# The same transformer kernel, with each engine's instructions ordered by another model of durations

## The chip, the cores and the metric

The program runs on one core of a Trainium2 chip. The metric is device time in microseconds. A core has separate instruction streams that run side by side and meet at semaphores: TensorE (PE, with its weight loads shown as PEld), VectorE (DVE), ScalarE (ACT), GpSimd (POOL) and SyncE (SP). SP here does nothing but issue DMA transfers; POOL issues some too. Within one stream the instructions run in the order in which they stand in the program.

## The reference

Input x has 4 sequences of 512 tokens with 128 channels. Four layers follow, each an attention part and a feed-forward part, with the layer norm behind each sum:

```python
for attn, ffn in layers:            # 4 layers
    x = layernorm(x + attn(x))
    x = layernorm(x + ffn(x))
```

- Layer 0: causal attention, 16 heads of 8 (`softmax(q k^T / sqrt(8) + causal) v`, then a projection); the feed-forward part is itself two small layers of local attention (8 heads of 64, window 64, normalised and rotated q and k) with a gated GELU network each.
- Layer 1: attention with relative positions (16 heads of 8; scores `(q k^T + q r^T + u k^T + v r^T)/sqrt(8)` with the terms in r shifted by row); feed-forward by 8 experts of which 2 are chosen per token.
- Layer 2: attention with a bias that falls linearly with distance (ALiBi), 16 heads of 8; a feed-forward network with ternary weights, 128 to 512 to 512 to 512 to 128.
- Layer 3: attention with 16 heads of 64 and tables of relative keys and values over distances from -16 to 16; feed-forward by 16 experts, 4 of them chosen in groups, and shared ones.

All arrays are float32. The output is x.

## The kernel before, in words

The residual stream x stays on the chip, one tile X per sequence of 128 x 4 x 128. `build` runs eight stages in one program: `Causal` (tiles named a0), `F0`, `Rel` (a1), `F1`, `Alibi` (a2), `F2`, `A3` and `F3`. Each stage is written as Python generators that take turns: `K.step` lets every generator that is open trace one more portion, `K.turn` hands out the PSUM banks for the smaller products, `K.tick` traces the next stage's preparation in the background. So the order in which instructions are traced already interleaves units of work.

That trace order is not yet the program's order. The tile context collects all instructions with their dependencies and then orders each engine's instructions itself. It walks through a modelled machine: at every point, among the instructions of an engine whose inputs the model has ready, it takes the one with the lowest priority number. The number is the place in trace order, which the kernel shifts in places. `K.front(800)`, for instance, puts the value matmuls ahead by 800, and the background has an offset of its own. What "ready" means at each point comes from modelled durations. Buffers of a pool and manual dependencies (`K.waits`, `K.behind`) are edges that any order keeps.

The causal and the ALiBi attention work in 16 units of 4 heads of one sequence:

- `load` (L518, L520): the operand tile Q of 256 KB and four blocks of rows of K of 64 KB each come back from DRAM (`a0iq`, `a0ik`) over SP, into one of `nb = 3` sets of buffers. `prep` had written them there by `spread` (L503) in three parts h, l of the float32 numbers; `ql` (L623) is the lower part. `constant` and `operands` (L479 to L494) fill the constant rows.
- `maxima` (L646 matmul, L648 on DVE): the scores by row, only to take the row maximum.
- `rows_out` (L664): the maxima are transposed, negated into the tile `nm`, and `mrow` (L532) writes them by DMA as one more row of Q, so that the second product of the scores comes out with the maximum subtracted.
- `exp` (L679 matmul into t, L723 exponent on ACT into Pt, L732 causal select on POOL), and the value matmuls (L695 into o), traced with `k.front(800)`. `exp` of a unit is traced only once its `rows_out` has been.

The relative attention `Rel` does the same with maxima at L922 to L927, scores at L996 to L998, the exponent at L999 and L1008, products on POOL at L1014 to L1018 and values at L972. `A3` works on one head of one sequence at a time: operand transfers on SP and POOL (L1235 to L1253; tiles a3Q, a3QT, a3K, a3KT, W), scores at L1285 and L1286, maximum L1290 on DVE, exponent p at L1291 on ACT, transposes by PE (L212 into t), the copy PT at L1304, a write of p to DRAM that is read back by diagonals (L1313 a3dpw, L1317 at), and values at L1334 under `k.front(800)`. `F0` has its projections near L1548 to L1610, scores at L1626, mask and maximum at L1639, exponent at L1641, transposes and copy at L1651, values at L1670, and its gated network at L1702 to L1765. `F1` has its expert outputs at L1952, `F2` its hidden products at L2053, `F3` its hidden part at L2200 to L2211 and its outputs at L2220. Weight tiles are split into an upper and a lower part by `split_w` (load into `wraw`, DVE at L295, POOL at L296), and products of such parts are three matmuls (`mm3`, L302 to L304).

## Time and profile before

| | us |
|---|---|
| median of 3 runs | 2275.97 (2273.09 to 2276.8) |
| profiled execution | 2282.43 |
| its span | 2280.7 |
| PE busy / DVE busy / ACT busy / POOL busy | 2028.8 / 1672.1 / 1333.8 / 589.0 |

The profiled execution is one run with the hardware profiler; its time is 1.7 us more than its span, and 6.5 us (0.28%) above the median. The granted clock of TensorE was 0.954 in it. The span is roughly: start to 55 us, causal attention to 190, F0 to 640, change of stage to 770, relative attention to 1095, F1 to 1255, ALiBi attention to 1455, F2 to 1600, A3 to 2150, F3 to the end. Neighbouring stages overlap at these borders. "Busy" counts the time in which an engine has an instruction in it, a waiting one among pipelined matmuls included; it is not the time at peak.

### The profile page before, as it was taken

What the parts mean: (1) busy time and instruction counts of PE and PEld (TensorE: products, weight loads), DVE (VectorE), ACT (ScalarE), POOL (GpSimd) and SP (SyncE); (2) the same over time, 40 slices, a digit from 0 to 9 for tenths busy, and PEclk for the clock granted to TensorE, in tenths of its full rate; (3) what the DMA queues carried; (4) which work ended last, traced back from release to release, by engine and by line L of the source; (5) the groups of instructions that cost most, each with busy time, mean ns of one, the idle gap of its engine ahead of it and who ended that gap; (6) DMA issues with size and microseconds to landing.
All of it is one profiled execution on the core that took longest, in us unless ns stands there. A gap on an engine that the chain in (4) does not pass through costs nothing.

```text
span 2280.7 us, 42119 instructions
## 1 busy us (share of the span) xinstructions
PE 2028.8 (89%) x13888; PEld 1473.5 (65%) x13888; DVE 1672.1 (73%) x5583; ACT 1333.8 (58%) x2982; POOL 589.0 (26%) x781
## 2 busy tenths in 40 slices
PE   5999787888778899999999999899899999999897
PEld 3666566666555566665788666677566666665676
DVE  4778688688978677874677787452778877778787
ACT  2566786677753456556342566332777776777632
POOL 3222212111222655555200222522111111111221
PEclk9999998899997899988999999999899999999999
DMA  6321311011341543420220330512889978898400
GB/s 183 91 78 34 101 47 47 22 28 30 112 130 54 165 141 116 143 75 23 69 65 9 108 106 30 167 54 57 211 204 217 206 192 184 199 216 197 118 5 15
DMA packets 265507, 242.31 MB, mean 106 GB/s; under 512 B 106368, under 2 KB 190634, under 8 KB 264522
## 3 DMA queue, kind: packets, MB, share of 16 engines
q1 hardware_dynamic: 260058, 222.12, 36.5%
q0 software_dynamic: 5232, 17.50, 3.3%
q8 instruction: 111, 1.82, 0.3%
q14 instruction: 106, 0.87, 0.1%
HBM read 103.03 MB, written 74.32 MB: 78 GB/s over the span
## 4 chain that ended last, share of the span: by engine, by line
PE 50%; DVE 13%; ACT 7%; DMA 5%; POOL 3%; issue 3%; SPq 1%; ACTq 0%; POOLq 0%; DVEq 0%
PE s L2053 4%; PE t L212 4%; PE o L1334 3%; PE o L972 3%; PE o L1952 2%; PE b L302 2%; PE s L302 2%; PE s L646 2%; PE t L679 2%; PE o L695 2%; PE s L303 2%; PE s L304 2%; PE b L303 2%; PE s L1285 2%; PE w L924 2%
## 5 line engine op out<-in xcount | busy, mean ns | idle before, releaser
L927 DVE CUSTOM_DVE_ANT_0 junk<-w,a1mask 128x640 bf16<-128x640 f32 x256 | 203.2, 817 | 67.8 <-PE w L925 66.8
L723 ACT ACTIVATE Pt<-t 128x384 f32<-128x384 f32 (+1 forms) x384 | 179.8, 529 | 74.8 <-PE t L679 62.6
L212 PE MATMUL t<-ident,p 128*128 128x128 f32 x1280 | 202.1, 278 | 21.0 <-ACT p L1291 15.6
L212 PEld LDWEIGHTS t<-ident,p 128*128 128x128 f32 x1280 | 150.8, 141 | 80.6 <-ACT p L1291 37.4
L999 ACT ACTIVATE Pt<-t 128x512 f32<-128x512 f32 x256 | 148.8, 597 | 84.2 <-PE t L998 44.3
L1304 ACT COPY PT<-t 128x512 f32<-128x512 f32 x256 | 149.7, 594 | 76.3 <-PE t L212 72.4
L1291 ACT ACTIVATE p<-s,nb 128x512 f32<-128x512 f32 x256 | 178.0, 700 | 13.0 <-DVE nb L1290 6.9
L1290 DVE TENSOR_REDUCE nb<-s 128x1 f32<-128x512 f32 x256 | 174.5, 685 | 2.5
L648 DVE CUSTOM_DVE_ANT_0 junk<-s,a0mask 128x128 bf16<-128x128 f32 (+3 forms) x256 | 114.0, 485 | 44.0 <-PE s L646 43.2
L1309 DVE CUSTOM_DVE_ANT_0 jk<-p,a3right 128x496 bf16<-128x496 f32 (+3 forms) x256 | 124.2, 485 | 26.9 <-ACT p L1291 16.0
L648 DVE CUSTOM_DVE_ANT_0 junk<-s,a2mask 128x128 bf16<-128x128 f32 (+3 forms) x256 | 114.9, 484 | 29.7 <-PE s L646 29.4
L732 POOL TENSOR_SCALAR_AFFINE_SELECT Pt<-Pt 128x512 f32<-128x512 f32 x112 | 70.9, 645 | 233.5 <-ACT Pt L723 233.4
L1288 DVE TENSOR_TENSOR s<-s,W 128x160 f32<-128x160 f32 (+1 forms) x256 | 80.9, 318 | 65.2 <-PE s L1286 64.3
L1285 PE MATMUL s<-a3KT,a3QT 128*128 128x512 f32 x256 | 118.5, 465 | 9.0 <-DMA a3K<-L 4.3
L1641 ACT ACTIVATE p<-sm,nb 128x128 f32<-128x128 f32 x256 | 100.7, 396 | 30.7 <-DVE nb L1639 30.0
L1334 PE MATMUL o<-PT,V 128*64 128x512 f32 x512 | 116.9, 598 | 0.5 <-ACT PT L1304 0.5
L996 PE MATMUL t<-a1Q,a1K 128*128 128x512 f32 (+3 forms) x256 | 96.5, 385 | 7.9 <-ACT Pt L999 5.3
L1286 PE MATMUL s<-a3K,a3Q 128*128 128x512 f32 x256 | 102.3, 400 | 0.0
L924 PE MATMUL w<-a1K,a1Q 128*128 128x256 f32 (+2 forms) x192 | 85.7, 447 | 14.1 <-DVE mx L927 13.1
L646 PE MATMUL s<-a0K,a0Q 128*128 128x256 f32 (+2 forms) x256 | 82.9, 380 | 16.6 <-DVE mx L648 8.0
L1639 DVE CUSTOM_DVE_ANT_0 sm<-s,band,rn 128x128 f32<-128x128 f32 x256 | 78.2, 343 | 24.1 <-PE s L1626 16.2
L1327 POOL CAST a<-at 128x256 fp32r<-128x256 f32 x32 | 12.9, 402 | 313.0 <-DMA at<-a3dpw 200.6
(494 smaller groups left out, 5927.3 us busy)
## 6 DMA issues: line engine op xcount, KB each, us to landing
W<-a3dsk SPq DMA_DIRECT2D x32, 640.0 KB
a1Q<-a1iq SPq DMA_DIRECT2D x32, 512.0 KB
a3dpw<-p SPq DMA_DIRECT2D x64, 160.0 KB
a3dpw<-p SPq DMA_DIRECT2D x64, 144.0 KB
a1K<-a1ik SPq DMA_DIRECT2D x64, 128.0 KB
a3Q<-a3dim SPq DMA_DIRECT2D x32, 256.0 KB
a3QT<-H SPq DMA_DIRECT2D x64, 128.0 KB
a3QT<-L SPq DMA_DIRECT2D x64, 128.0 KB
```

The lines of the kernel that those rows point to most:

```text
L212: self.nc.tensor.matmul(out.bitcast(x.dtype), x, i[:n, :n], is_transpose=True, start=start, stop=stop)
L646: self.scored = nc.tensor.matmul(s[:, :nm], self.qof(0, t, i)[:, qc * P:(qc + 1) * P], Ks[:, i, :nm], start=True, stop=True).ins
L648: nc.vector.tensor_tensor_reduce(junk[:, :n], s[:, :n], k.mask[:, 512 - n:512], 1.0, NEG, ALU.add, ALU.max, mx[:, qc, i:i + 1])
L723: ready = nc.scalar.activation(Pt[:, i, z:], s[:, z:], AF.Exp, scale=sc).ins
L924: nc.tensor.matmul(s[:, 0, T - n:], self.qof(0, t, i)[:, qs], Ks[:, i, 0:n], start=True, stop=True)
L927: nc.vector.tensor_tensor_reduce(junk, s.rearrange("p a n -> p (a n)")[:, T - n:T + m], k.mask[:, T - n:T + m], 1.0, NEG, ALU.add, ALU.max ...
L999: nc.scalar.activation(Pt[:, i, :T], s, AF.Exp, scale=sc)
L1285: nc.tensor.matmul(s, QT[:, e, qs], KT[:, e, :], start=True, stop=False)
L1290: nc.vector.tensor_reduce(nb, s, AX.X, ALU.min)
L1291: nc.scalar.activation(p[:, e, :], s, AF.Exp, bias=nb, scale=-1.0, accum_out=den[:, qc, 2 * un + e:2 * un + e + 1])
L1304: self.copied[t] = nc.scalar.copy(PT[e][:, :, qc * P:qc * P + P], tb.rearrange("p (c n) -> p c n", n=P)).ins
L1334: m = nc.tensor.matmul(o[64 * e:64 * e + 64, :], V[:, kc, h * 64:h * 64 + 64], PT[e][:, kc, :], start=(kc == 0), stop=False)
```

## The change

One argument is given to the tile context. The context then walks through its modelled machine with its other model of durations (a timeline simulation) when it orders the instructions of each engine. Trace order, priorities, dependencies, tiles and arithmetic stay as they were; which instruction counts as ready at which point, and so the order on each engine and the semaphore waits that go with it, can come out otherwise.

```diff
-    with tile.TileContext(nc) as tc:
+    with tile.TileContext(nc, schedule_with_timeline_sim=True) as tc:
         build(tc, aps, range(8))
```

## The prediction

> **What bounds the kernel now.** I read the page's busy shares first, then the chain that ended last, the waits of PE and last the start of the timeline; the windows by stage gave the sizes.
>
> ```profile
> PE 2028.8 (89%) x13888; PEld 1473.5 (65%) x13888; DVE 1672.1 (73%) x5583; ACT 1333.8 (58%) x2982; POOL 589.0 (26%) x781
> ...
> PE 50%; DVE 13%; ACT 7%; DMA 5%; POOL 3%; issue 3%; SPq 1%; ACTq 0%; POOLq 0%; DVEq 0%
> ```
>
> PE is busy 89% of the span, yet only 50% of the chain is matmul time. The other half is a softmax step on DVE or ACT, a transfer, or the moment before a matmul that nothing explains. So the order in which PE meets results of other engines is worth time, though no engine's work changes.
>
> ```profile
> 1600.00:2150.00 550.00, 514.89 (x2879) 342.60 (x2879) 427.19 (x1247) 409.54 (x962) 71.60 (x127) 0.99 0.84 199
> 190.00:640.00 450.00, 369.82 (x3624) 280.64 (x3623) 362.34 (x1292) 323.39 (x890) 88.67 (x108) 0.93 0.21 54
> ```
>
> Two of the windows (length; PE, PEld, DVE, ACT, POOL busy; clock; DMA share; GB/s): the relative-key attention (A3) leaves PE idle 35 us, the local attention (F0) 80 us of 252 in all. DVE and PE are equally loaded in F0, so an order that is better for PE can be worse for DVE there.
>
> ```profile
> PE t L212 <- ACT p L1291: 15.6, 24, 1.6
> PE s L646 <- DVE mx L648: 14.1, 26, 2.5
> ...
> PE s L646 <- DMA a0K<-a0ik: 7.9, 1, 7.9
> PE b L302 <- DVE ql L623: 7.8, 1, 7.8
> ...
> PE t L679 <- DMA a0Q<-nm: 4.6, 3, 2.6
> ```
>
> PE's waits (us, times, longest): no matmul waits for an operand load of the causal attention (a0Q, a0K) after the first one, and only 3 of 16 units wait for the row of maxima (nm). Those loads are in time now; I watch whether they stay so.
>
> ```profile
> 15.60 0.75 DVE L623 SCALAR_TENSOR_TENSOR ql<-b,a0bqk,qh 128x512 fp32r<-128x512 f32 x1 [8.68 <-DMA a0ik<-a0c]
> 23.81 7.67 SPq L520 DMA_DIRECT2D a0K<-a0ik  x12
> 29.63 2.35 PE L646 MATMUL s<-a0K,a0Q 128*128 128x256 f32 x6 [7.88 <-DMA a0K<-a0ik]
> ```
>
> The start is one dependent run: fills on SP, ql, loads, first maxima at 29.6 us.
>
> **The change, part by part.** It removes and adds no matmul, activation of data or transfer; it permutes each engine's list. Beside that, ACT loads its activation table once more (41 times for 40; such a load takes 1.28 us at L316, and I count it as hidden, ACT being idle 42% of the time; 1.3 if it is not), and the instructions that only wait go from 801 to 690 on PE and from 662 to 695 on SP, which I cost at nothing but their place. I compared the two orders: the matmuls fall into 7799 runs of equal instructions before and 7727 after, the mean matmul moves by 2.3 us of PE work, score matmuls (L646, L924, L1626) come earlier by 3 to 4 us, value matmuls (L972, L1334, L1952, L2220) later by 2 to 4. To price this I give every instruction the mean duration that its group has in the trace and measure **room**: the PE work between the matmul that feeds another engine (or the place where a transfer can be issued) and the matmul that uses the result. Room below the steps in between is **shortfall**, a wait. One late result delays all behind it, so sums of shortfalls overstate; what part I take is judgement.
>
> *Start.* POOL now has two a0K memsets (1.77 us each, from 5.30 for three) ahead of the identity's select (which stood at 1.64), and further memsets ahead of a0wqkl. SP has table and weight loads of F0 ahead of the fills and spreads that ql and the first load wait for. Followed by hand with the rows' durations, ql moves from 15.6 to about 21, the first maxima from 29.6 to about 35. Nothing hides this, PE has no other work. +6 (0 if the transfers overlap, to 10).
>
> *Causal attention.* Maxima run earlier, so each Q load of 256 KB (L518) is needed sooner after its buffer comes free. Room from issue to first use: 3.5 to 9.8 before, median 6.4; after, unit by unit from the fourth, 6.7, 7.3, 5.8, 7.5, 3.9, 1.8, 2.0, 2.5, 2.0, 0.7, 1.1, 0.3, 0.8. The nearest row for such a load is "a3K<-in_c_step_dram POOLq DMA_DIRECT2D x2, 256.0 KB, 5.2", so the shortfalls are 1.3+3.4+3.2+2.7+3.2+4.5+4.1+4.9+4.4 = 32, less about 2 that exist now: 30. PE still has values and exponent matmuls of older units there; I take two thirds, 20. The nm row (L532) needs some 2.1 from issue: the chain shows 2.68, 2.50 and 1.77 for a2Q<-nm. Its room falls from a median of 2.9 to 1.2: 16 x 0.9 = 14, of which 4.6 is paid now; most falls into the same delays, 3 more. +23 (8 if other matmuls cover, 40 if not).
>
> The Trainium skill, "DMA: Bandwidth & Descriptors", section "Anatomy of one DMA — SWDGE (gpsimd) path", fits a transfer as 2.0 us plus its bytes over 436e3. By it the 256 KB load would be an estimated 2.6 us, the shortfalls 10 instead of 32 and this term about +8; the 5.2 us row disagrees, and the row decides. The rule is also one against the change: 2 us that do not shrink are more than the 1.2 of room left to nm.
>
> *Alibi attention.* Q loads keep their room (15.7, now 17). nm's median room falls from 3.3 to 1.6, below 2.1 in about 11 units by 0.6: +7 (0 to 12).
>
> *A3.* Value matmuls stand further behind their last PT copy (room 1.0, now 2.0; the copy is 0.59), transposes behind the exponent 4.0 instead of 3.8. Shortfalls as PE sees them go from 90 to 54 us, as DVE sees them from 125 to 73. But PE's recorded waits for the exponent are only 15.6, and the chain in this stage is 5.9% a3dpw<-p, 5.1% a3Q<-H and 3.2% L1253: loads that a better order of matmuls does not shorten. Their median room grows (a3KT 4.8 to 8.0, a3K 5.5 to 7.9), its lowest tenth shrinks (3.1 to 1.8, 3.6 to 2.8), because SP interleaves loads with writes of p. Of the 36 saved I take a little over half: -20 (-45, with part of DVE's 52, to +5).
>
> *F0.* Transposes after the exponent get 4.4 instead of 2.9; PE's shortfalls fall from 139 to 86, DVE's rise from 173 to 192. The 53 on PE is nearly given back where DVE, as loaded as PE, is the one that waits: -5 (-35 to +20).
>
> *The rest.* Rel: value room 2.9 to 4.0, PE's shortfalls 105 to 116: -3 (-12 to 8). F1's clean alternation of 12 hidden and 8 out matmuls is broken up, shortfalls 3 to 9: +3. F2 2 to 4: +1. F3's room after h falls from 5.1 to 2.7, shortfalls 5 to 15, half of it masked: +4.
>
> Sum: 6+23+7-20-5-3+3+1+4 = +16. The profiled execution took 2282.43, 6.5 above the median of 2275.97; applied to it the sum is 2298, and on the median **2292**.
>
> **Rivals.** *Faster.* The matmuls' longer distance from ACT and DVE in A3 and F0 decides: A3 -40, F0 -25, Rel -8, and the causal loads are mostly covered (+10 with nm), start +3, the rest +10: -50, about 2226 at its end, 2250 in its middle. For it speak the shortfalls on PE and that L1334 and L972 gain a whole microsecond; against it that the recorded waits these would remove are small (15.6 for p, 8.5 for POOL's Pt) and that DVE's shortfalls in F0 grow. It wins as soon as A3 and F0 together bring more than the 44 of the other terms.
>
> *Same, about 2276.* PE is 89% busy, and moves by 2.3 us could disappear in what stands between. The Trainium skill, "Perfetto Trace Analysis", opening note, calls matmul busy time "a bad metric, because matmuls are pipelined" and points to the load of weights: here 65%, against PE's 89%. By the page there is much room for order to matter, by the 89% row little; the chain's 50% agrees with the page. An exact balance of gains and losses remains possible.
>
> *Much slower, about 2340.* SP serves its list in order: a load placed behind a write that waits for p holds up all loads behind it. If the Q loads of the causal unit come late in full (+40) and A3 gains nothing for that reason (+5) while F0 pays on DVE (+15) and the rest stays, the sum is near +75. For it speaks that SP's waits on PE grow from 159 to 225 instructions; against it the larger median room of the A3 loads.
>
> **How the numbers follow.** Measurement tells about 0.2%, 4.6 us, from no change. The forecast (2281 to 2335) has 0.50, much slower 0.13, same 0.10, faster 0.27. The terms that rest on recorded durations most firmly, the causal loads and the start, are losses; the gains rest on counts that overstate. The range 2253 to 2335 leaves out the far end of the faster case (0.08) and of the slowest (0.12). The slower cases alone, with most of the chance, span 2281 to 2340.
>
> **What would show it.** Right: first maxima near 35 us; new PE waits for a0Q<-a0iq, of 15 us or more in all; more than three waits for a0Q<-nm; the causal stage ending 20 to 40 us later; A3 shorter by 10 to 30, with the wait of t on p below 10 us. Wrong: no wait for the Q loads, or a longer A3 with SP queue rows in its chain. If F0 moves by over 35 us either way, my weighing of PE against DVE there was the failed step.

## The result, and the profile after

The changed kernel takes 2367.06 us (median of 4 runs, 2361.83 to 2369.53) against 2274.86 us of the kernel before (4 runs): ratio 1.0396, 95% interval 1.0377 to 1.0415. It is slower by 92 us, where 16 were forecast. The profiled execution of the changed kernel has a span of 2363.8 us.

The page's busy shares and the engines' shares of the chain that ended last, changed kernel:

```profile
PE 2059.0 (87%) x13888; PEld 1511.8 (64%) x13888; DVE 1684.4 (71%) x5583; ACT 1325.6 (56%) x2983; POOL 587.3 (25%) x781
...
PE 53%; DVE 17%; DMA 12%; ACT 11%; issue 4%; SPq 2%; POOL 0%; ACTq 0%; DVEq 0%; POOLq 0%
```

All engines have the same instructions, but for one more table load on ACT, and nearly the same busy times (DVE 12 us more, ACT 8 less, PE 30 more for the same 13888 matmuls, at a granted clock of 0.932 against 0.954). The chain's shares can't be set beside those of the kernel before as they stand: those add up to only 82%, because that chain breaks off at 383 us and nothing ahead of that is in it. From the last matmul of F0 (L1760) to the end, which both chains cover, it is in transfers for 96 us before and 198 after, in ACT for 91 and 114, in DVE for 226 and 207, in POOL for 65 and 5, in PE for 967 and 944. So what grew is above all the time in transfers.

Cutting both traces at the same matmuls shows where the time went (us, from the starts of the first and last matmul of a line):

| stage, up to the last | before | after | difference | forecast |
|---|---|---|---|---|
| start, to the first L646 | 29.6 | 32.2 | +2.6 | +6 |
| causal attention, L679 | 216.4 | 242.9 | +26.5 | +23 |
| F0, L1760 | 506.6 | 531.0 | +24.4 | -5 |
| relative attention, L972 | 337.0 | 315.5 | -21.5 | -3 |
| F1, L1952 | 160.5 | 165.0 | +4.5 | +3 |
| ALiBi attention, L695 | 187.5 | 194.6 | +7.1 | +7 |
| F2, L2053 | 148.2 | 144.4 | -3.8 | +1 |
| A3, L1334 | 565.7 | 594.9 | +29.2 | -20 |
| F3, end | 129.2 | 143.3 | +14.1 | +4 |
| sum | 2280.7 | 2363.8 | +83.1 | +16 |

The windows of A3, cut in this way, kernel before and then the changed kernel (length; PE, PEld, DVE, ACT, POOL busy; granted clock; DMA share; GB/s):

```profile
1585.80:2151.50 565.70, 524.69 (x2933) 349.70 (x2931) 435.44 (x1279) 411.90 (x966) 73.92 (x132) 0.99 0.84 198
```

```profile
1625.60:2220.50 594.90, 530.00 (x2933) 363.26 (x2931) 430.15 (x1279) 408.08 (x966) 75.05 (x134) 0.95 0.79 189
```

The same 2933 matmuls run in a stretch that is 29 us longer; DVE and ACT are busy for less time than before. So the stage lost time to waits. Which ones, PE's waits in the changed kernel say first:

```profile
PE s L1285 <- DMA a3KT<-H: 15.1, 5, 8.0
PE t L212 <- ACT p L1291: 14.4, 17, 3.6
...
PE t L679 <- DMA a0Q<-nm: 7.5, 9, 2.6
PE s L646 <- DMA a0Q<-a0iq: 7.4, 4, 2.9
PE b L302 <- DVE ql L623: 7.1, 1, 7.1
PE t L679 <- DMA a2Q<-nm: 6.9, 10, 1.2
```

Three rows are of the forecast kind: waits for a0Q<-a0iq are new (7.4 us, where I had asked for 15 or more), those for the nm rows of a0 went from 3 to 9 and of a2 from 3 to 10. The first row was not forecast: score matmuls of A3 now wait up to 8 us for an operand load, and the wait of the transposes for p, which I wanted below 10 us, has stayed.

### The profile page after: what moved, and what is told of

Same layout as the page of the kernel before. It is cut to its first block, busy times and chain, and to the rows that moved or that the text cites. A ratio compares the mean times of both kernels' runs of the same rounds, so it can differ in the third digit from the quotient of the medians.

```text
span 2363.8 us, 42073 instructions
## 1 busy us (share of the span) xinstructions
PE 2059.0 (87%) x13888; PEld 1511.8 (64%) x13888; DVE 1684.4 (71%) x5583; ACT 1325.6 (56%) x2983; POOL 587.3 (25%) x781
## 4 chain that ended last, share of the span: by engine, by line
PE 53%; DVE 17%; DMA 12%; ACT 11%; issue 4%; SPq 2%; POOL 0%; ACTq 0%; DVEq 0%; POOLq 0%
PE t L212 4%; PE s L2053 4%; PE t L679 4%; PE o L695 3%; PE o L1334 3%; PE s L646 3%; PE o L972 3%; PE o L1952 2%; DMA a3Q<-H 2%; ACT p L1641 2%; PE b L212 2%; PE s L302 2%; PE s L304 2%; PE s L303 2%; PE t L996 2%
## 5 line engine op out<-in xcount | busy, mean ns | idle before, releaser
L212 PE MATMUL t<-ident,p 128*128 128x128 f32 x1280 | 205.3, 285 | 29.6 <-ACT p L1291 14.4
L1291 ACT ACTIVATE p<-s,nb 128x512 f32<-128x512 f32 x256 | 180.1, 706 | 38.9 <-DVE nb L1290 29.6
L1309 DVE CUSTOM_DVE_ANT_0 jk<-p,a3right 128x496 bf16<-128x496 f32 (+3 forms) x256 | 124.1, 485 | 26.2 <-ACT p L1291 21.2
L1334 PE MATMUL o<-PT,V 128*64 128x512 f32 x512 | 117.2, 600 | 1.4 <-ACT PT L1304 1.4
L1288 DVE TENSOR_TENSOR s<-s,W 128x144 f32<-128x144 f32 (+1 forms) x256 | 79.3, 317 | 44.0 <-PE s L1286 42.8
L646 PE MATMUL s<-a0K,a0Q 128*128 128x256 f32 (+2 forms) x256 | 87.1, 402 | 22.4 <-DMA a0K<-a0ik 7.8
L1639 DVE CUSTOM_DVE_ANT_0 sm<-s,band,rn 128x128 f32<-128x128 f32 x256 | 75.1, 345 | 37.2 <-ACT p L1641 21.2
L1249 DVE TENSOR_TENSOR L<-b,H 128x512 fp32r<-128x512 f32 x64 | 43.9, 687 | 74.5 <-ACT H L1248 45.9
```

Of the source, the lines that this page charges most:

```text
L212: self.nc.tensor.matmul(out.bitcast(x.dtype), x, i[:n, :n], is_transpose=True, start=start, stop=stop)
L646: self.scored = nc.tensor.matmul(s[:, :nm], self.qof(0, t, i)[:, qc * P:(qc + 1) * P], Ks[:, i, :nm], start=True, stop=True).ins
L1291: nc.scalar.activation(p[:, e, :], s, AF.Exp, bias=nb, scale=-1.0, accum_out=den[:, qc, 2 * un + e:2 * un + e + 1])
L1334: m = nc.tensor.matmul(o[64 * e:64 * e + 64, :], V[:, kc, h * 64:h * 64 + 64], PT[e][:, kc, :], start=(kc == 0), stop=False)
```

## The experiments

The order of a stage can be carried from one kernel to the other by itself. I took the places in trace order of each engine's instructions from the changed kernel, and in the kernel before I added an edge (issue order only, no wait) between neighbours of that list, for the instructions traced while one stage runs:

```diff
+def pin(tc, nc):
+    ins = list(nc.cur_bb.bb.instructions)
+    info = mybir.DependencyInfo(mybir.DependencyClass.NoSync, mybir.DependencyReason.DATA)
+    for o in PINS:                    # one list per engine: places in trace order
+        for a, b in zip(o, o[1:]):
+            tc.add_manual_dep(ins[b], ins[a].name, info, reason="order")
...
         build(tc, aps, range(8))
+        pin(tc, nc)
```

The stage so pinned has the changed kernel's order on all five engines, and all other stages have that of before, but for places at the borders, where two stages interleave. The runs below are named for the stage with the new order.

### Each stage by itself

Edit: PINS hold the new order of A3; of F0; of the relative attention; of the start and the causal attention; of F1, ALiBi, F2 and F3 together.

> The kernel before, with only the instructions traced during stage A3 (all five engines) put into the order that the changed kernel has; every other stage keeps the order of before. From the start of F2's end to A3's last value matmul the changed kernel takes 594.9 us against 565.7. Theory 1 (each stage's own order makes its loss): +25 to +35 us on the whole. Theory 2 (the loss is handed on from earlier stages, by the lower granted clock and by transfers that start later): under +10 us.

> The kernel before, with only stage F0's instructions in the order of the changed kernel. Between the last scores of the causal attention and F0's last network matmul the changed kernel takes 531.0 us against 506.6, but the relative attention behind it overlaps and is 21.5 us shorter there. Theory 1 (own order): +15 to +30. Theory 2 (handed on): under +8. If F0's loss and Rel's gain are one and the same shift of work across the border: near 0 here and near 0 for Rel.

> The kernel before, with only the instructions traced during the relative attention in the order of the changed kernel. Theory 1 (own order): -15 to -22 us, a version faster than both kernels. Theory 2 (Rel only made up for a late F0): -5 to +5.

> The kernel before, with only the start and the causal attention in the order of the changed kernel. Theory 1 (own order; late Q loads and nm rows): +25 to +32, of which about 3 at the start. Theory 2 (later stages take the delay up): under +10.

> The kernel before, with F1, the ALiBi attention, F2 and F3 in the order of the changed kernel. The four single-stage runs so far sum to +55 us (causal +30, F0 +26, A3 +22, Rel -23) and the whole change is +92. Theory 1 (each stage's own order, stages independent): the rest is +15 to +25 by the traces (F1 +4.5, ALiBi +7.1, F2 -3.8, F3 +14.1), and some 15 us come from the stages meeting each other. Theory 2 (no interplay): +37.

| run | median us | ratio to before | interval | times 2276 us |
|---|---|---|---|---|
| causal_new | 2310.89 | 1.0131 | 1.0104 to 1.0158 | +30 |
| f0_new | 2306.59 | 1.0112 | 1.0084 to 1.0141 | +25 |
| rel_new | 2257.94 | 0.9892 | 0.9856 to 0.9929 | -25 |
| a3_new | 2303.08 | 1.0102 | 1.0072 to 1.0133 | +23 |
| rest_new | 2311.68 | 1.0128 | 1.0086 to 1.0170 | +29 |

(Runs of before differ from one group of runs to the next by up to 0.5%, so I go by ratios within a group.) The five differences sum to 3.65%, 83 us, of the whole change's 3.96%. So every group of stages loses or gains by its own order; what is left, some 7 us, is within the intervals. Cut at the same matmuls as above, the pinned stage takes nearly what it takes in the changed kernel (causal attention 242.6 us, F0 530.8, relative attention 316.2, A3 589.2), and no other stage differs by more than 5 us from before. So the loss is not, in the main, a delay that is handed on from stage to stage. F0's loss and the relative attention's gain are two things, not one shift of work. rel_new is faster than both kernels. Two sizes lie outside what was expected: A3 just under its band of 25 to 35, the relative attention's gain above its 15 to 22; and rest_new's 29 lies between its two theories. In rest_new F3 takes 143.8 us, as in the changed kernel, F1 (160.3) and F2 (148.1) are as before, and the ALiBi attention takes 205.3 (187.5 before), more than in the changed kernel itself (194.6), with a2Q<-nm at 11.9% of its chain. So these four do meet each other; how was not followed, and no run takes F3's loss apart.

### The causal attention: which transfers

Edit, beside the pinned new order of the stage, with the row of maxima in the second run only:

```diff
-        for v in range(self.NV):      # load: Q, L518; mrow: nm, L532
+        for v in range(self.NV if self.nm != "a0" or t < 3 else 0):
```

> As causal_new, but the Q loads (L518) of the fourth to the last unit of the causal attention are left out, so that these units use old queries. Theory 1 (the Q loads cost the 20 us that the prediction's term has): the +30 us falls to about +10. Theory 2 (the trace of the changed kernel has a0Q<-a0iq with 12.3 us on the chain and nm with 20.6): +15 to +20 remain.

> As the one before, and the writes of the row of maxima (L532) of the same units are left out too, so that their exponents are shifted by old maxima. If Q loads and nm rows are the whole loss of the causal stage: within 5 us of the order of before without the same transfers, the start's 3 us apart. If the order of maxima and exponents costs by itself: 10 us or more above it.

> The control: the order of before everywhere, without the same Q loads and rows of maxima. 0 to 10 us faster than before, since PE waits 4.6 us there for nm and never for a Q load behind the start.

Measured: ratio 1.0047 (1.0030 to 1.0064) without Q loads, 1.0035 (1.0020 to 1.0050) without both, and 0.9983 (0.9957 to 1.0010) for the control. From 1.0131 the Q loads account for 0.84%, 19 us (some 7 either way by the intervals), and the nm rows for another 0.12%, 3 us, which the intervals do not tell from nothing. The first came down to about the +10 that theory 1 gave it. Against the control, which is itself 4 us under before, 0.52%, 12 us, are left, of which 3 us are the start. So the two kinds of transfer are most of the loss but not all of it: the order of maxima and exponents, or its meeting with F0, has the rest. The changed kernel's chain in this stage had these transfers at other prices:

```profile
by line: PE t L679 17.9%; PE o L695 14.6%; PE s L646 14.1%; DMA a0Q<-nm 8.5%; PE b L212 7.7%; issue 5.3%; DMA a0Q<-a0iq 5.1%; DVE junk L648 4.5%; ACT Pt L723 2.8%; PE b L302 1.8%; ACT nm L664 1.6%; PE b L303 1.5%; PE b L304 1.5%; DMA a0iq<-
```

5.1% of 242.9 us are 12 us for the Q loads, which cost 19; 8.5% are 21 us for the nm rows, which cost 3. PE's waits in the new order without these transfers:

```profile
PE s L646 <- DMA a0K<-a0ik: 9.0, 1, 9.0
PE b L212 <- DVE a0ot L747: 7.9, 6, 2.2
PE s L646 <- DVE mx L648: 5.9, 21, 0.6
```

Waits for a0Q are gone from the top; what stays is the one wait at the start and small ones on DVE.

### A3: the transfers of the operands

Edit: the twelve loads of a unit left out from the third unit on, under the new order of A3 and under the old.

```diff
-                for dst, s in ((QT[0:64], H), (QT[64:P], L), (Q2[0:64], H)) if i == 0 else ((KT[0:64], H), ...
+                for dst, s in () if t > 1 else ((QT[0:64], H), (QT[64:P], L), (Q2[0:64], H)) if i == 0 else ((KT[0:64], H), ...
```

> As a3_new, but the operand transfers of A3 (L1253, twelve for each unit) are left out from the third unit on, so that the scores use old operands. Nothing then waits for them: neither the matmuls L1285 and L1286 nor the copies H and L, whose two buffers the transfers read. Theory 1 (the loss of A3 is these transfers: ScalarE and VectorE stand at H and L until a transfer has read the buffer, and the first score matmul of a unit waits): within 4 us of the order of before without the same transfers. Theory 2 (the order of matmuls, exponents and reductions by itself): still 15 to 25 us slower than that one.

> The control: the order of before everywhere, with the same operand transfers of A3 left out from the third unit on. 20 to 60 us faster than before, as the chain there holds some 8 to 10% of 566 us of them.

Measured: 2257.61 us, ratio 0.9885 (0.9853 to 0.9918), in the new order; 2270.75 us, 0.9940 (0.9921 to 0.9959), in the old. In the traces the stage takes 539.6 against 556.6 us. So without its loads the new order of A3 is the faster one, by 13 to 17 us; the loads cost it 2.17%, 49 us, and the old order 0.6%, 14 us. The loss of A3 is these transfers, as theory 1 has it, and without them the new order is not merely level with the old. The control gained less than the 20 to 60 us that I had read from its chain. The chain's lines in A3, before and then in the changed kernel:

```profile
by line: PE o L1334 13.3%; PE t L212 12.6%; PE s L1285 6.4%; PE s L1286 5.9%; DMA a3dpw<-p 5.7%; DMA a3Q<-H 5.0%; ACT p L1291 4.3%; PE b L302 4.2%; PE b L1388 4.1%; DVE nb L1290 4.0%; issue 3.9%; SPq L1253 3.1%; PE b L303 2.8%; PE b L304 2.
```

```profile
by line: PE o L1334 10.9%; PE t L212 9.8%; DMA a3Q<-H 8.5%; DMA a3KT<-H 6.0%; PE s L1285 5.8%; ACT p L1291 5.3%; PE s L1286 4.8%; DVE nb L1290 4.8%; PE b L1388 4.2%; issue 4.1%; DMA a3QT<-L 3.7%; DMA a3K<-L 3.6%; SPq L1253 3.0%; ACT PT L130
```

Loads from H and L with their issue (L1253) hold 8.1% of 566 us before in the rows listed, 46 us, and 24.8% of 595 us after, 148 us. So the chain has the direction right, and three times the price.

ScalarE's waits show how, for A3 in the kernel before and then in a3_new:

```profile
ACT PT L1304 <- PE t L212: 72.4, 73, 4.3
...
ACT p L1291 <- DVE nb L1290: 6.9, 14, 1.0
ACT H L1248 <- DMA a3KT<-H: 3.9, 1, 3.9
ACT H L1248 <- DMA a3Q<-H: 3.6, 7, 1.0
```

```profile
ACT PT L1304 <- PE t L212: 42.2, 44, 3.4
ACT H L1248 <- DMA a3Q<-H: 38.3, 14, 5.4
ACT p L1291 <- DVE nb L1290: 32.1, 41, 3.2
ACT H L1248 <- DMA a3KT<-H: 15.5, 3, 11.3
```

H is a tile in two buffers: a projection is copied into it, and four transfers read it from there. The two copies of a unit stand close together on ScalarE in both orders. In the new one the next unit's copies often follow sooner (with fewer than 15 other instructions of ScalarE between the pairs at 14 of 31 places, before at 8), when transfers of the earlier pair have not yet read their buffers. ScalarE takes its instructions in order, so it stands at H for 54 us in all, where it was 7.5, and the exponents behind it stand too. The runs without loads show what the transfers cost, not that all of it passes through H: PE's waits for a3KT<-H, at the scores, fall with them from 15.9 to 8.1 us, and a wait of 11.3 us at H at the start of the stage, for the loads that remain, stays. A run with a third buffer of H, which would tell, was not made.

### A3: is it SP's order?

In the new order SP has writes of p, which wait for exponents, between the loads that read one H. Edit: only SP's list of a3_new is changed, with the loads of one pair H, L together at the place of the first (Q, q, K, k are loads from H, "-" from L, w writes of p, the others further transfers of the stage):

```diff
-KK--wwQ-qwmWQ-wqKK--RwwQ-qKwmWQ-qwK--R
+KK--wwQ-qQ-qwmWwKK--RwwQ-qQ-qKK--wmWwR
```

> As a3_new (+22 us), with one engine's list edited: SP issues all six loads that read one pair of H and L tiles together, at the place of the first of them; in the changed kernel's order writes of p, which wait for exponents, stand between them. Theory 1 (H and L stay occupied behind those writes, ScalarE and VectorE wait for H and L, and the exponents behind that): the loss falls to between -13 and +8 us. Theory 2 (the loads are slow because DMA engines are busy, or are asked for too late by PE's list): +15 to +25 stay.

> The relative attention in the changed kernel's order together with A3 as in a3_new_grouped, all else as before. If stages are independent: the sum of -23 us and of what a3_new_grouped shows.

Measured: 1.0113 (1.0080 to 1.0147), no better than a3_new. Theory 1 fell, and ScalarE's waits say where the time went:

```profile
ACT p L1291 <- DMA a3dpw<-p: 34.0, 21, 4.3
ACT p L1291 <- DVE nb L1290: 28.5, 40, 3.4
ACT H L1248 <- DMA a3KT<-H: 20.1, 7, 10.6
ACT H L1248 <- DMA a3Q<-H: 13.9, 8, 4.2
```

The wait for a3Q<-H fell from 38.3 to 13.9, but p now waits 34.0 us (5.1 in a3_new) until a write has read its buffer: writes stand behind loads instead of loads behind writes. One wait was exchanged for the other. So this other arrangement of SP's list does not remove the loss. I read it so, without a run for it: the projections come at a time when SP's queue has not room for loads and writes both. The DMA engines are not busier there (share 0.79 in the changed kernel's A3, 0.84 before). Why the transfers of one unit need that much longer was not separated further. The two stages together gave 2280.3 us, 1.0014 (0.9996 to 1.0033), the sum of +26 and -25.

### The relative attention: the distance of the value matmuls

Edit in the kernel before, builder's first model:

```diff
-    nb, lead, lag, ahead = 3, 6, 4, 3
+    nb, lead, lag, ahead = 3, 6, 6, 3
```

> The kernel before with the builder's first model, and one number of the source changed: lag of the relative attention from 4 to 6 slots, so that value matmuls are traced later behind their exponents. Their room behind the last product on POOL becomes 5.0 us in the median (before 2.9, changed kernel 4.0). Theory 1 (Rel gains because its value matmuls no longer wait for POOL's products, which hold some 9 to 10% of its chain before and no visible part in rel_new): -10 to -22 us. Theory 2 (it gains from the order of score matmuls and of DVE's maxima): -3 to +3.

Measured: 2262.57 us, ratio 0.9914 (0.9886 to 0.9943), -20 us, as theory 1 has it. In this run's trace PE's wait for POOL's products (L972 for L1018) is 1.9 us, where it was 8.5. The builder orders the rest of the stage anew when the number changes, and the run does not separate that. The chain's lines in the relative attention, kernel before and then rel_new:

```profile
by line: PE o L972 16.0%; PE t L996 7.8%; PE w L924 7.7%; PE w L925 5.9%; DVE junk L927 5.9%; issue 5.8%; POOL Pt L1018 5.7%; PE t L1007 5.5%; ACT Pt L999 4.0%; PE t L998 3.7%; POOL Pt L1017 3.5%; PE b L212 2.4%; PE b L892 1.8%; ACT Pt L100
```

```profile
by line: PE o L972 15.3%; PE t L996 9.6%; PE w L924 7.4%; DVE junk L927 7.0%; PE w L925 6.8%; PE t L1007 6.6%; issue 5.1%; PE t L998 4.5%; ACT Pt L999 3.8%; DMA a1K<-a1ik 3.7%; PE b L212 2.8%; PE b L892 2.0%; DMA a1Q<-a1iq 1.9%; SPq L503 1.
```

POOL's products (L1018 5.7%, L1017 3.5% of 367 us, 34 us) have left the listed part of the chain; the loads a1K<-a1ik and a1Q<-a1iq (5.6% of 349 us, 20 us) took part of their place. PE's own wait for the products was only 8.5 us in 14 cases before, and the 25 us gained are three times that. I read it so, without a run for it: a value matmul that waits 0.6 us also delays the next scores, and with them the next exponents that POOL needs.

### F0: three theories

Edits, each with the new order of F0. First, ScalarE left out of the pinned lists. Then the scores on a constant tile, new and old order:

```diff
-                    m = nc.tensor.matmul(self.s[e][o:o + 64, c * P:c * P + P], qT[r, pr, ...], kT[r, pr, ...], ...)
+                    m = nc.tensor.matmul(self.s[e][o:o + 64, c * P:c * P + P], self.sel[r, c, o:o + 64].bitcast(F32), self.sel[r, c, :].bitcast(F32), ...)
```

Last, two buffers of masked scores, new and old order:

```diff
-        sm = pool.tile([P, 4, P], F32, tag="sm", name=f"sm{u}{h}", bufs=self.ns)
+        sm = pool.tile([P, 4, P], BF16, tag="sm", name=f"sm{u}{h}", bufs=2)
```

> The kernel before, with F0's instructions on PE, DVE, POOL and SP in the order of the changed kernel; ScalarE's order there is left to the builder's first model (about half of its instructions then stand elsewhere than in the changed kernel). Theory 1 (the copies and squares of the next projections stand ahead of ready exponents on ScalarE and hold them up): the +26 us falls to +13 or less. Theory 2 (PE's and DVE's own lists make the loss): +20 to +30.

> As f0_new (+26 us), but the score matmuls of F0 read a constant tile in place of the projected, rotated and transposed q and k; all other work is done as before, only the scores no longer wait for it. Theory 1 (the new order brings the operands of the next unit late, so that DVE's rotation steps lie on the path): within 8 us of its control f0_old_oldops. Theory 2 (the loop of exponents, transposes and values, or the gated network, loses by itself): 15 us or more above it.

> The control: the order of before everywhere, with the same score matmuls on a constant tile. 0 to 15 us faster than before.

> As f0_new (+26 us), but the masked scores sm of F0 are kept in bfloat16 (rounded, which changes the output a little) in two buffers instead of one in float32, in the same memory. VectorE then no longer stands at sm until ScalarE has read the head before; that wait is 21.2 us in f0_new against 6.5 before. Theory 1 (late exponents on ScalarE hold up VectorE through the one sm buffer, and its operand and network steps behind that): the loss over its control falls to between 5 and 14 us. Theory 2 (ScalarE itself stands at results of the projections L1569, L1572 and at transposes L1610, and VectorE's wait is only its shadow): 20 us or more stay.

> The control: the order of before everywhere, with the same two bfloat16 buffers sm. 0 to 6 us faster than before, the wait there being 6.5 us.

| run | median us | ratio to before | interval |
|---|---|---|---|
| f0_free_act | 2344.43 | 1.0264 | 1.0232 to 1.0296 |
| f0_new_oldops | 2303.70 | 1.0117 | 1.0079 to 1.0154 |
| f0_old_oldops | 2276.77 | 0.9995 | 0.9974 to 1.0015 |
| f0_new_sm2 | 2296.40 | 1.0066 | 1.0045 to 1.0087 |
| f0_old_sm2 | 2270.47 | 0.9954 | 0.9938 to 0.9970 |

In each pair the theory that named a cause fell. A ScalarE order that the first model chooses around the other engines' new lists is worse still, +60 us, which neither theory had. With scores that wait for no operands, 1.22%, 28 us, remain between new and old order: late q and k are not the cause. With two buffers sm (of a narrower type, so two things change), VectorE's wait for the exponent (21.2 us in f0_new) is gone from the list of its waits, both orders gain about 10 us, and 1.12%, 25 us, remain between them. What the trace of f0_new shows beside that, in ScalarE's waits:

```profile
ACT kT L1610 <- PE t L212: 24.1, 23, 5.6
ACT ta L1569 <- PE b L304: 19.8, 9, 6.9
ACT sq L1572 <- DVE ss L1579: 15.8, 13, 3.4
ACT p L1641 <- DVE nb L1639: 14.5, 11, 4.3
```

Before, the second and third were 4.9 and 7.6 us and the wait of p for nb was 28.7: ScalarE stood at exponents whose scores were not ready; now it stands at projections that are not ready, with exponents behind them. With sm2 these rows are 10.3 and 14.6 us in the new order and the loss is the same, so this is a reading and not a cause shown. Between the first exponents of successive units the new order takes 9.3 us more at the first unit, 5.6 at the one where the weights change and 13.9 at the last, and 11 less in the four others together. With the scores on a constant tile the places are the same (10.2, 9.6 and 14.1 more, 15.7 less in the four others). So the loss lies at the first and the last unit and where the layer changes, and the steady units gain; which list makes it stays open.

## Why the prediction was wrong, point by point

**The causal attention was right in mechanism; that the size fits is in part luck.** Q loads were put at 20 us and cost 19; nm rows on top at 3 and cost 3; the whole with the start at 29 and was 29 in the trace, 30 by itself. But the term has nine late loads of 5.2 us each, a row of POOL's queue. The trace has four waits for Q loads, and the chain has these loads, which SP issues, at 2.7 to 3.3 us each from issue to use. With 3.1 us the same sum of shortfalls would be 14 and two thirds of it 9 (an estimate from these rows). So late Q loads cost more than their own lateness, and a duration that was too long made up for that. The start took 2.6 of its 6 (ql at 18.2 us instead of 21, first maxima at 32.2 instead of 35), and some 9 us that I had not named lie in the new order of maxima and exponents, or in its meeting with F0.

The Trainium skill's fit in "DMA: Bandwidth & Descriptors", section "Anatomy of one DMA — SWDGE (gpsimd) path", is stated there for transfers that GpSimd issues. Its estimate for 256 KB, 2.6 us, is nearer to the 2.7 to 3.3 us of SP's four loads than my row of 5.2 is. The 8 us of the term that I worked out from it are further from the measured 22 than my 23.

**A3 is the step that failed most: -20 forecast, +23 by itself.** The gain that I read from the larger room of PE and DVE is there: 13 to 17 us, once the loads are left out. What failed is the sentence on the loads, where I took the median room of the load at its consumer, saw it grow, and counted the loads only as time that would not be gained. I looked at who reads the destination and not at who needs the source free again. The loads cost 49 us where they cost 14, and the wait that grew most sits at the copy H on ScalarE, in front of the exponents.

**F0: -5 forecast, +25.** I set PE's shortfall (53 us less) against DVE's (19 more) and took nearly a draw. The order by itself lies, in its middle, above the upper bound of +20 that I had given. The counts looked at pairs of one result and one use; what they leave out was not found, and the cause stays open.

**The relative attention: -3 forecast, -25.** The mechanism named (value matmuls farther behind their Pt) was right and is supported by rel_lag6. The size was off because I weighed the 8.5 us of recorded wait and a rise in PE's count (105 to 116), and not the 34 us that POOL's products held on the chain.

**F1, ALiBi, F2 and F3** were put at +15 and make +22 in the changed kernel, +29 by themselves. F3 has the difference: 14 for 4. ALiBi's 7.1 for 7 agree in the changed kernel, with the waits for nm that were forecast; but its stage costs 17.8 in rest_new, and no run leaves its nm rows out, so the agreement may be luck.

**The rivals.** "Much slower" was the right one in sign and in its mechanism, transfers on SP held up, and too small: its terms sum to about +75, and it named about 2340, which is +64. What it missed was F0's 25, where it had 15, that A3 pays not only for lost gains, and F3. "Same" rested on PE's busy share, which fell from 89% to 87% while the kernel lost 4%. The Trainium skill's "Perfetto Trace Analysis", opening note, that matmul busy time is a bad metric, agrees with this case in that the same 13888 matmuls were busy for 2028.8 us before and 2059.0 after; but the share of the weight loads, to which it points, moved as little (65% to 64%). My reading that only half of the chain is matmul time was wrong: the chain covers 1894 of the 2280.7 us, and PE has 1131 us of these, 60%.

The range ended at 2335, which is +59. The upper ends of its own terms (10, 40, 12, 5, 20 and 8, and 8 for the three small ones) sum to +103, about 2379; I had held it unlikely that they come together. Four groups of stages lost 23 to 30 us each, A3 and F0 more than their upper ends, and only the relative attention gained.

## What to carry to other kernels

When an order changes, look at three edges of every transfer: when its data is needed, when its destination comes free, and when its source does. A copy into a tile of few buffers that transfers read belongs on an in-order engine only at a place where those transfers are over. Then do not take a recorded wait for a price, and the chain's share of the producer not either. Here is what both said, beside what leaving the work out gained (for the nm rows, with the Q loads out already; for POOL's products, what the two better orders gained):

| | recorded wait, us | on the chain, us | measured, us |
|---|---|---|---|
| Q loads, causal attention, changed order | 7.4 (PE) | 12 | 19 |
| nm rows, causal attention, changed order | 7.5 (PE) | 21 | 3 |
| operand loads of A3, changed order | 54 (ScalarE at H) | 148 | 49 |
| operand loads of A3, order of before | 7.5 (ScalarE at H) | 46 | 14 |
| POOL's products, relative attention, before | 8.5 (PE) | 34 | 20 to 25 |

The measured cost is above the recorded wait in three rows and below it in two; the chain has too much in four rows and too little in one. Only a run without the work tells. A builder's other model is not better or worse as a whole; pinned stage by stage it gave +30, +25, -25 and +23 us, and +29 for the four other stages together, and most of the one gain could be had in the source by a single number.

## What was not expected of the hardware

The granted clock of TensorE fell in the stages that became longer. In A3 it was 0.99 before and 0.95 in the changed kernel, in F3 0.99 and 0.91, over the whole span 0.954 and 0.932; in the relative attention, which became shorter, it rose from 0.90 to 0.92. Between stages it does not follow PE's idle share: F3 before is idle for 16% at 0.99, the relative attention for 10% at 0.90. The last windows, F3 before and then after:

```profile
2151.50:2280.70 129.20, 108.90 (x646) 89.31 (x642) 110.36 (x370) 39.87 (x62) 29.15 (x54) 0.99 0.05 14
```

```profile
2220.50:2363.80 143.30, 116.76 (x646) 97.14 (x642) 116.26 (x370) 41.46 (x63) 24.79 (x52) 0.91 0.04 12
```

These means are a mixture: in every trace here the granted clock is at each moment either the full or half of it. In F3 it is at half for 3.6 us before and for 26.5 after, in A3 for 13.7 and 54.6, in the whole program for 212 and 324. The same 646 matmuls of F3 are busy for 7.9 us longer. In the 18 traces that keep F3's order of before, the stage has 3.6 to 14.6 us at the half clock and takes 129.1 to 133.8 us, about 0.4 us more for each us at half (a line through these 18). Carried on to 26.5 us, that would be some 9 of F3's 14 us, an estimate beyond the range of these runs. So part of what a wait costs may be paid by matmuls that do not wait themselves. How much of the 92 us that is, and whether the waits make the clock fall, no run here separates.
